# Column width of the routed experts' products, and where the routing tables are allotted

## The chip, the cores and the metric

The kernel runs on one core of a Trainium2 chip. The metric is the device time of one execution in microseconds (us); times below are medians of several executions. All data are fp32. The engines are TensorE (PE in the profile; its weight loads are shown apart as PEld), VectorE (DVE), ScalarE (ACT), GpSimd (POOL) and SyncE (SP, which issues most of the DMAs).

## The reference, cut to what matters

The reference is a decoder of two layers on `x` of 8 batches of 256 tokens with 256 features. Each layer has self attention, cross attention and a feed-forward part, each added to `x`. The change touches the end of layer 1: the start of its mixture of experts lies beside the last cross attention, and its routed experts are the last stage of the program. The mixture of experts, for 2048 tokens, 8 experts and F = 704:

```python
scores_aE = x_aD @ router_DE
vals_aK, idx_aK = jax.lax.top_k(scores_aE, K)                       # K = 1
gates_Ea = jax.nn.sigmoid(masked_aE).T                              # 0 for all other experts
routed_in_EaD = gates_Ea[:, :, None] * x_aD[None, :, :]
mid_EaF = silu(einsum('ead,edf->eaf', routed_in_EaD, w1_eDF)) * einsum('ead,edf->eaf', routed_in_EaD, w3_eDF)
routed_out_EaD = einsum('eaf,efd->ead', mid_EaF, w2_eFD)
shared_aD = silu(x_aD @ ws1_DF) * (x_aD @ ws3_DF) @ ws2_FD
out_aD = shared_aD + routed_out_EaD.sum(axis=0)
```

Since only one expert has a gate other than zero for a token, the kernel computes one expert per token.

## The kernel before, in words

The program works through the stages one after the other: layer 0, the self attention of layer 1, the cross attention of layer 1 with one batch at a time, and then the mixture of experts. A scheduler orders the instructions of an engine by priorities; where `tc.manual_schedule` is open, the engines it names keep the order in which the code records them. PE is under such a hand-written order around the projections of the cross attention (L1586, L1588) and in the stages after it, SP during the routed stage (L1884).

**Cross attention (`null_cross_attention`, from L1288).** For batch `b` the loop at L1568 records the scores (`stx`, L1431), their exponentials (`pTx`, L1435), the sums `both` (L1437, POOL), the denominators `den` (L1446) and the weighted values `ox` (L1470). While batch `b` is in work, the keys, values and queries of batch `b + 1` are made by `seven` (tiles `k`, `v`, `q`, products at L276). In the last batch there is no next batch, and the shared network of the experts takes that place: `load_shared` (L1054) loads `ws13` (weights ws1 and ws3, two DMAs at L1028 and L1029, and a small copy on POOL at L1030) and clears the tails of `mid0`, `mid1` and `ws2` (L1035, POOL); `hidden_shared` makes the first quarter of the shared hidden layer (`hx`, L1079), and DVE makes sums of the weights (`tws`, L1091). The reciprocals of the denominators (`rx`, L1490 and L1491, DVE) go to DRAM (`rd`, L1497) and back, spread over the partitions (`rs`, L1501); then `oT` is multiplied by them (L1525, POOL and DVE) and projected (`wo`, L276).

**Pools.** The projection weights of the cross attention and the keys, values and their sums lie in pools on the right side of SBUF that belong to `wproj`. `wproj.close()` at L1582 gives the room back, and the pool `mids` is opened in it. A first write into a new pool waits for the last readers of what lay in its room. In the kernel before, `mids` holds `ws13`, `mid0`, `mid1`, `ws2` and, by `routing_tables(late)` at L1604, all tables of the routing: index rows, `lower`, `run`, `sums`, `at`, `rank`, `hot`, `before` and some columns.

**Routed stage (`token_experts`, from L1644; loop in `slots`).** The tokens have been sorted by expert into 17 tiles of 128 rows. Twelve of them (numbers under `PAIRED` = 12) are full tiles of one expert. Five (12 to 16) are half tiles: 64 rows of one expert and 64 of another, with two sets of weights. They are taken in the order 0, 1, 12, 2, 3, 13, and so on. For each tile, SP loads `w13` (1408 KB for a set, L1808) two tiles ahead and `w2` (768 KB, L1815) one tile ahead, each kind with four buffers, so that a load waits until PE has read what lay in its buffer. Two tiles at a time are transposed on PE (`xrp`, L1824). `into` makes the hidden layer of the tile that comes next: 11 blocks of 128 hidden features, with two blocks of 128 input features each. `outof` multiplies the hidden layer (`midr`) by `w2`: 6 blocks into an output of 256 features (`out`, L1846). So PE runs `into` of tile i + 1 and then `outof` of tile i.

In `into` the products go through the helper `product` (L274 to L278), which splits the 128 columns of the stationary operand into two instructions of 64 columns that write partitions 0 to 63 and 64 to 127 of the output:

```python
nc.tensor.matmul(out[h], lhsT[:, h], rhs, start=start, stop=stop, skip_group_check=True)
for h in (slice(0, 64), slice(64, P))
```

`outof` splits in the same way. In a full tile both halves multiply the same `w2`; in a half tile each half, the 64 rows of one expert, multiplies its own. In `into` a half tile's 64 rows are the moving operand, so that its products have 128 columns of weights and 64 columns of tokens, once for each set. The hardware runs every fp32 product as two passes, each with a weight load of its own, so the profile counts twice the instructions that the code has: 88 for a full tile's `into`, 176 for a half tile's, 24 for `outof`.

After the last tile PE makes the last quarter of the shared network (`h`, L1079, and `out`, L1663), while POOL gathers the routed rows, and DVE adds them to `x`.

## Time and profile before

| | |
|---|---|
| median of 3 executions | 1196.16 us (1195.59 to 1197.24) |
| the profiled execution, its own time | 1198.71 us |
| its span, from the first to the last instruction | 1197.0 us |
| mean granted TensorE clock | 0.992 of full speed |
| PE busy | 1135.5 us, 95% of the span |
| weight loads busy | 706.5 us, 59% |
| DVE, ACT, POOL busy | 566.2, 447.5, 417.6 us |
| chain that ended last, by engine | PE 76%, POOL 7%, issue 6%, DVE 6%, ACT 4%, DMA 1% |
| `h` at L276, first products of the routed tiles | 87.0 us busy, 1936 passes |
| `out` at L1846, second products of the routed tiles | 47.1 us busy, 408 passes |

The profile is one execution. Busy times are unions of the records of an engine; the ends of matmuls are modelled and overlap, so the time that a group really takes is the distance between the start of its first instruction and the start of the next group, which the chain and the timelines show. The chain of waits follows the work back from the last instruction, at each step to what released it. In the lists of groups a line such as L276 may be that of a helper. A shape such as 128*64 128x128 gives the stationary operand (128 rows, 64 columns) and the moving one (128 rows, 128 columns).

### The profile page before, as it was taken

Reading aid. Unit: us, or ns where it says so; the run is one execution under the profiler, and the core shown is the slowest. Engines: PE = TensorE matmul, PEld = TensorE weight load, DVE = VectorE, ACT = ScalarE, POOL = GpSimd, SP = SyncE. Lnnn points to the kernel's source line nnn. Section 1 sums busy time; section 2 is a strip of 40 time slices with the busy share of each in tenths; the row PEclk is TensorE's granted clock in tenths of the full one; section 3 lists DMA queues with packets and bytes.
Section 4 is the critical chain, followed back from the end, with each engine's and each line's share of the span. In section 5 each row is a group of like instructions: output and inputs, shape, how many; then the busy total and the mean of one; then the engine's idle time right before and its main releaser. Section 6 shows DMA issues by size and latency. Waiting matters only on the chain.

```text
span 1197.0 us, 31939 instructions
## 1 busy us (share of the span) xinstructions
PE 1135.5 (95%) x13788; PEld 706.5 (59%) x13788; DVE 566.2 (47%) x1564; ACT 447.5 (37%) x696; POOL 417.6 (35%) x482
## 2 busy tenths in 40 slices
PE   6898899998899999999999999999998999999996
PEld 2334444454445454666676767666664576888864
DVE  5465878778685643824241424242324473222213
ACT  3666665665443541314141414141413230222220
POOL 3245365455655730314141414141415114100013
PEclk9999999999999999999999999999998999999999
DMA  7046232130200600020202010101103007799924
GB/s 226 1 133 204 91 119 92 54 122 2 84 2 17 233 3 19 2 54 2 54 2 54 6 50 10 46 19 37 24 15 105 5 30 305 277 414 394 392 73 129
DMA packets 51446, 116.78 MB, mean 98 GB/s; under 512 B 8272, under 2 KB 36416, under 8 KB 46944
## 3 DMA queue, kind: packets, MB, share of 16 engines
q1 hardware_dynamic: 45120, 98.90, 24.0%
q0 software_dynamic: 3456, 12.73, 2.9%
q10 hardware_dynamic: 2720, 3.02, 0.7%
q8 instruction: 110, 1.80, 0.6%
q14 instruction: 40, 0.33, 0.1%
HBM read 104.00 MB, written 27.93 MB: 110 GB/s over the span
## 4 chain that ended last, share of the span: by engine, by line
PE 76%; POOL 7%; issue 6%; DVE 6%; ACT 4%; DMA 1%; SPq 0%; POOLq 0%; ACTq 0%; DVEq 0%
PE h L276 7%; PE k L276 6%; PE v L276 6%; PE wo L276 5%; PE ox L1470 5%; PE stx L1431 5%; PE st L334 4%; PE out L1846 4%; PE o L371 3%; PE out L1663 3%; PE h L1079 3%; PE qk L282 3%; PE q L276 3%; ACT pT L345 2%; PE den L1446 2%
## 5 line engine op out<-in xcount | busy, mean ns | idle before, releaser
L345 ACT ACTIVATE pT<-st 128x1024 f32<-128x1024 f32 (+1 forms) x128 | 110.7, 919 | 64.3 <-PE st L334 64.3
L371 PE MATMUL o<-pT,padv 128*32 128x256 f32 (+1 forms) x1536 | 99.7, 370 | 4.3 <-POOL pT L350 4.2
L371 PEld LDWEIGHTS o<-pT,padv 128*32 128x32 f32 x1536 | 40.6, 109 | 86.2 <-issue 37.5
L1437 POOL TENSOR_TENSOR both<-pTx 128x512 f32<-128x512 f32 x64 | 81.2, 1296 | 29.0 <-ACT pTx L1435 23.8
L276 PE MATMUL h<-xrT,w 128*64 128x128 f32 (+1 forms) x1936 | 87.0, 250 | 0.4 <-issue 0.4
L276 PEld LDWEIGHTS h<-xrT,w 128*64 128x64 f32 x1936 | 84.4, 137 | 3.3 <-issue 1.1
L345 ACT ACTIVATE pT<-st,kbias 128x1024 f32<-128x1024 f32 x64 | 67.9, 1112 | 44.0 <-PE st L334 44.0
L258 POOL TENSOR_TENSOR lnrs<-lnve,mhalf 128x2 f32<-128x2 f32 x48 | 34.7, 723 | 127.8 <-DVE lnve L256 124.1
L1072 DVE TENSOR_TENSOR midr<-sl,h 128x128 f32<-128x128 f32 x102 | 29.4, 288 | 102.5 <-PE h L276 69.9
L1435 ACT ACTIVATE pTx<-stx 128x1024 f32<-128x1024 f32 x64 | 62.1, 1022 | 40.8 <-PE stx L1431 27.7
L1071 ACT ACTIVATE sl<-h 128x128 f32<-128x128 f32 (+1 forms) x114 | 35.4, 311 | 94.7 <-PE h L276 55.7
L334 PE MATMUL st<-qm,kT 32*128 32x512 f32 (+1 forms) x512 | 66.8, 591 | 4.0 <-ACT pT L345 2.0
L1431 PE MATMUL stx<-qTx,kTx 64*128 64x256 f32 x512 | 64.4, 391 | 2.5 <-ACT pTx L1435 2.5
L282 PE MATMUL qk<-l_wqkv,xnT 128*32 128x512 f32 x512 | 63.3, 607 | 0.7 <-ACT xnT L294 0.7
L1470 PE MATMUL ox<-pTx,vx 128*64 128x256 f32 x512 | 62.3, 385 | 0.0
L258 POOL TENSOR_TENSOR lxrs<-lxve,mhalf 128x2 f32<-128x2 f32 x8 | 5.6, 706 | 159.9 <-DVE sc L1210 124.2
L1525 POOL TENSOR_TENSOR oT<-oT,rs 128x512 f32<-128x512 f32 x30 | 37.3, 1273 | 65.0 <-DMA rs<-rd 65.0
L1431 PEld LDWEIGHTS stx<-qTx,kTx 64*128 64x128 f32 x512 | 46.1, 186 | 20.3 <-ACT pTx L1435 7.2
L276 PE MATMUL wo<-wout_x,oT 128*64 128x256 f32 x512 | 58.0, 379 | 0.0
L350 POOL TENSOR_SCALAR_AFFINE_SELECT pT<-pT 128x512 f32<-128x512 f32 x64 | 42.0, 670 | 41.8 <-ACT pT L345 38.7
L1846 PE MATMUL out<-w,midr 128*64 128x256 f32 x408 | 47.1, 379 | 2.7 <-issue 2.7
L1470 PEld LDWEIGHTS ox<-pTx,vx 128*64 128x64 f32 x512 | 33.9, 136 | 26.4 <-issue 12.5
(361 smaller groups left out, 2164.1 us busy)
## 6 DMA issues: line engine op xcount, KB each, us to landing
w<-packs SPq DMA_DIRECT2D x22, 1408.0 KB
w<-packs SPq DMA_DIRECT2D x22, 768.0 KB
rs<-rd SPq DMA_DIRECT2D x16, 512.0 KB
packs<-L_ffn_w_eDF SPq DMA_DIRECT2D x8, 704.0 KB
packs<-L_ffn_w_eDF SPq DMA_DIRECT2D x8, 640.0 KB
packs<-L_ffn_w_eFD SPq DMA_DIRECT2D x8, 640.0 KB
ctxT<-ctx_T SPq DMA_DIRECT2D x8, 512.0 KB
wkv_x<-L_xattn_Wkv POOLq DMA_DIRECT2D x1, 4096.0 KB
```

The source lines that it names most:

```text
L258: nc.gpsimd.tensor_tensor(rs[:, :n], ve[:, :n], mhalf[:, :n], ALU.pow)
L276: nc.tensor.matmul(out[h], lhsT[:, h], rhs, start=start, stop=stop, skip_group_check=True)
L282: nc.tensor.matmul(out[h : h + HP], lhsT[:, h : h + HP], rhs, start=start, stop=stop, skip_group_check=True)
L334: nc.tensor.matmul(st[:, r, :, :n], self.kT[rows, c, bass.ts(kt, P)], self.qm[rows, :, c, q0:], start=True, stop=True,)
L345: nc.scalar.activation(pT[:, :, :, :n], st[:, 2 * k : 2 * k + 2, :, :n], AF.Exp, scale=self.scale, **kb)
L350: nc.gpsimd.affine_select(out=pT[:, :, :, :P], in_=pT[:, :, :, :P], compare_op=ALU.is_ge, fill=0.0, base=0, pattern=[[0, 2], [0, 2], [1, P ...
L371: nc.tensor.matmul(o[HP * j : HP * j + HP, m, q0:], self.v_pad[:, kt, 8 * c + 2 * j + m, :], pTs[j // 2][:, j % 2, m, : S - q0], start=kt ...
L1431: nc.tensor.matmul(st[:, g, kt, :], kT[rows, c, bass.ts(kt, P)], qT[rows, c, :], start=True, stop=True)
L1435: nc.scalar.activation(pT, st, AF.Exp, scale=scale)
L1437: nc.gpsimd.tensor_tensor(both, pT[:, :, 0, :], pT[:, :, 1, :], ALU.add)
L1470: nc.tensor.matmul(o[XD * g : XD * (g + 1), i, :], v[:, kt, 2 * (c2 + i) + g, :], pT[:, g, kt, :], start=kt == 0, stop=kt == 1, skip_group ...
L1846: nc.tensor.matmul(ps[h], mid[:, i, h], sets[k % len(sets)][1][:, i, :], start=i == 0, stop=i == NFC - 1, skip_group_check=True,)
```

## The change

The first part opens a pool `route` after `mids` and allots the routing tables in it, so that `mids` becomes smaller. The second part writes the first products of all routed tiles with all 128 columns of weights in one instruction, and the second products of full tiles too. The second products of half tiles keep their two halves, since these have different weights.

```diff
                 late = ctx.enter_context(tc.tile_pool(name="mids", bufs=1, side="right"))
+                tables = ctx.enter_context(tc.tile_pool(name="route", bufs=1, side="right"))
                 load_shared(late)
                 sums = phase.enter_context(tc.tile_pool(name="sums", bufs=1, side="right"))
...
                 w_out(shared["ws2"], a["L1_ffn_ws2_FD"])
-                routing_tables(late)
+                routing_tables(tables)
...
             def first(h, lo):
                 for i, (w13, _) in enumerate(sets):
                     for c in range(2):
-                        product(h[:, bass.ts(i, n)], w13[:, c, lo : lo + P], xrT[:, c, bass.ts(i, n)], c == 0, c == 1)
+                        nc.tensor.matmul(
+                            h[:, bass.ts(i, n)],
+                            w13[:, c, lo : lo + P],
+                            xrT[:, c, bass.ts(i, n)],
+                            start=c == 0,
+                            stop=c == 1,
+                            skip_group_check=True,
+                        )
...
             for i in range(NFC):
-                for k, h in enumerate((slice(0, 64), slice(64, P))):
+                for k, h in enumerate((slice(0, 64), slice(64, P)) if len(sets) > 1 else (slice(0, P),)):
                     nc.tensor.matmul(
```

## Prediction

> **What bounds the kernel now.** I read the page first: TensorE (PE) is busy 95% of the span and holds 76% of the chain that ended last. A busy PE need not be at its limit, so I then read the chain of waits in order of time at the two places that the diff touches, the granted clock there, the weight loads (PEld) by shape, and the timelines of single groups. First place: the start of the shared network in the last batch of the cross attention (start us, length us, what).

> ```profile
> 915.49 4.35 DMA ws<-L_ffn_ws_DF
> 919.84 0.14 issue
> 919.98 6.62 PE hx L1079 x8
> 926.60 0.57 PE sc L276 x16
> 927.17 10.50 PE hx L1079 x24
> ```

> The load of ws13 is issued only at 915.49, and PE is idle for it from 916.56 to 919.98 (3.42 us). What follows is slow too: eight hx passes take 6.62 us where 24 take 10.50, 0.4375 each, so eight should take 3.50. The stretches tell why (stretch, length, busy us of PE, PEld, DVE, ACT, POOL, granted clock, DMA share, GB/s): after the pause PE runs at half clock.

> ```profile
> 918.00:920.00 2.00, 0.02 (x1) 0.06 (x1) 2.00 (x5) 0.00 (x0) 1.06 (x5) 0.77 1.01 397
> 922.00:924.00 2.00, 2.00 (x4) 0.83 (x3) 2.00 (x3) 0.00 (x0) 0.00 (x0) 0.50 1.14 360
> ```

> Second place: the routed stage, 1021 to 1158 us, again in the chain.

> ```profile
> 1042.20 0.59 PE xrp L1824 x4
> 1042.79 4.95 PE h L276 x88
> 1047.74 2.59 PE out L1846 x24
> 1050.34 4.80 PE h L276 x88
> ...
> 1130.43 5.13 PE h L276 x176
> 1135.56 2.10 issue
> 1137.65 2.81 PE out L1846 x24
> ```

> Each fp32 product is two passes, and each pass is today a pair of 64-column instructions side by side; I call the pair a slot. First products of a full tile: 4.80 / 44 = 109.1 ns a slot (128 tokens stream through). Of a half tile: 5.13 / 88 = 58.3 ns (64 tokens). Second products: 2.59 / 12 = 215.8 ns (256 columns). The middle of this stage:

> ```profile
> 1060.00:1098.00 38.00, 37.00 (x684) 33.19 (x682) 8.37 (x29) 10.40 (x35) 2.14 (x4) 1.00 1.00 401
> ```

> DMA is full as well, and PE waits for weights three times: the second products at 1063.60 last 3.37 us until the next group (2.59 undisturbed), the half tile at 1082.50 lasts 5.83 (5.13), and 2.10 are waited at 1135.56; together 3.6 us.

> What decides the case is the weight load by its width (line, shapes, count, busy us, mean ns, idle before):

> ```profile
> L282 PEld LDWEIGHTS back<-ys,put 128*32 128x32 f32 x256 | 8.7, 110 | 5.3 <-issue 0.7
> L276 PEld LDWEIGHTS h<-xrT,w 128*64 128x64 f32 x1936 | 84.4, 137 | 3.3 <-issue 1.1 <-ACT yr L1855 1.0 <-ACT sl L1071 0.2
> L1663 PEld LDWEIGHTS out<-ws,mid 128*128 128x128 f32 x192 | 36.3, 190 | 6.2 <-issue 1.0 <-ACT spx L1154 0.5
> ```

> From 32 to 64 columns a load grows by 27 ns, from 64 to 128 by 53: 0.83 ns a column. So 64 columns need 53 ns of loading and 128 need 106. A half tile's slot of 58.3 is the 64-column load and 5.3 ns, not the streaming: it is bound by loads, which two column halves make at once. And one place already runs 128-column fp32 products on short streams (start us, length us):

> ```profile
> 969.62 0.38 PE L1265 MATMUL counts<-hot,ones 128*128 128x128 f32 x2
> 969.84 0.39 PE L1266 MATMUL counts<-hot,lower 128*128 128x128 f32 x2
> 970.06 0.28 PE L1267 MATMUL counts<-low,ones 128*128 128x1 f32 x2
> ```

> and its weight loads:

> ```profile
> 969.95 0.30 PEld L1267 LDWEIGHTS counts<-low,ones 128*128 128x128 f32 x2
> ```

> Two passes over 128 tokens every 0.22 us, so 0.11 a slot. The last two loads cover 0.30 us, one lasts 0.19 (mean 192 ns): they start 0.11 apart although one column streams.

> [...]

> **The change part by part.**
> *First products of full tiles.* 12 tiles x 44 slots. By the load rule a 128-column slot is 106 + 5.3 = 111.3 ns (the counts show 0.11) instead of 109.1: +2.2 x 528 = +1.2 us. Bounds: 0, if streaming still sets it, and +1.6 at 112 ns.
> *First products of half tiles.* 5 tiles x 88 slots. 64 tokens still stream, but each slot has to load 128 columns through one path: 111.3 instead of 58.3 ns, +53.0 x 440 = +23.3 us. No product of 128 columns over 64 tokens is in the trace; bounds are 109 and 114 ns from the counts (+22.3 to +24.5), and, should loads overlap further, 58.3, that is no cost (first rival).
> *Second products of full tiles.* A 128-column pass over 256 columns in the shared products takes 18.13 / 84 = 215.8 ns (L1663 in the chain at 1000.24), the same as a pair today: 0. Its 106 ns load lies beside 216 ns of streaming.
> *Second products of half tiles* are unchanged.
> *Mode changes.* A turn into 64-column mode costs 0.15 us (4.95 - 4.80), a turn out 0.15 (four transposes 0.59 us against 0.43 at 1018.21, within 128-column mode). Before: one entry, eight rounds around transposes, one exit, 18 x 0.15 = 2.7. After: only around the second products of five half tiles, 10 x 0.15, and some 0.05 more each time the 128-column load comes back, 1.7. So -1.0 us (0 to -1.5).
> *Weight waits.* PE becomes slower while the 22 loads of each kind stay as they are, so the 3.6 us of waits go: -3.6 (0 to -3.6). What is late next is PE itself.
> The stage: +1.2 + 23.3 - 1.0 - 3.6 = +19.9 us.
> *Tables in their own pool.* In the built program ws13's load waited for the last ox product (done at 915.4); now it waits for the last product of batch 7's q (L276 q, ends at 895.5). So it is issued 20 us earlier into idle DMA queues and lands near 900 (4.35 us before). PE's pause and its half clock go: -(3.42 + 6.62 - 3.50) = -6.5 us. What moves with it: (a) SP: both parts of ws2 go ahead of rd; they wait for nothing after 895.5, and rd is due at 918.5. (b) POOL: three memsets (1.24 us at 915.5) move before lxrs and wait for the same q; ready at 896.8, when lxrs (896.84) is due. Behind them stand the normalization and the sums "both", for which den waits; a copy of 0.29 us also goes between these. The first two sums end at 905.3, 0.8 us before den at 906.07, so 0.4 us of delay is covered; without cover it would cost 0.4. (c) DVE: a tws of 0.74 us replaces an sx of 0.33 between rx and its reciprocal, so rd leaves 0.4 us later; in return rs no longer shares the queues with ws. Batch 6 needed 8.9 us from rd to oT (862.26 to 871.15), batch 7 11.1 (918.54 to 929.63). With 8.9 POOL's oT are ready at 930.4; wo now starts at 931.1. With 11.1 the second would be due 932.6, needed at about 933. Covered, by little: 0 to +1.
> All of the chain after 926 is PE's, or hangs on PE's products, and shifts along.

> Sum: +19.9 - 6.5 = +13.4 us. The profiled execution took 1198.71 us with a span of 1197.0, 2.55 above the median, so it should become 1212.1; from the median of 1196.16, 1209.6 us.

> **The rivals.** *Main case (0.85)*: as worked out. Bounds: +22.3 + 0 - 1.5 - 3.6 - 6.5 = +10.7, and +24.5 + 1.6 + 0 - 2.6 - 5.5 = +18.0 with 1 us of weight waits and 1 us of new stalls at wo left; 1207 to 1214.
> *Faster: loads of 128 columns hide behind short products (0.10).* Place: the half tiles' first products, at 58 to 60 ns a slot. For it: a wide load lies under a running product everywhere else, and transposes at 109 ns a slot (0.43 / 4) show no load cost at all. Against it: that stream is 128 long, and the L1267 loads keep 0.11. Then PE gains nothing, DMA stays the bound of the stage, and -6.5 to -7.5 remain: 1189. It decides below 81 ns a slot: there 440 x (81 - 58.3) = 10.0 us equals the 6.5 + 3.6 + 1.0 - 1.2 of gains.
> *The earlier load doesn't pay (0.03):* den or wo takes the place of the ws13 wait, and the pause returns there. Then +19.9: 1216. Against it are the margins above.
> *The clock falls in half tiles (0.02),* where only 64 of 111 ns stream: some of 49 us at half clock, 1225 and more. Against it: clock 1.00 at 58.3 ns slots today.

> **How the numbers follow.** The likeliest case gives 1209.6. Its bounds, 1207 to 1214, widened by 2 at the low end for the faster case's flank (a slot between 81 and 109), make the range 1205 to 1214; it leaves out the rivals, 0.15, and little of the main case. A difference under 0.2% (2.4 us) can't be told from none here. Faster by more: 0.10. Within: 0.02, a slot near 81 ns. Slower by more: 0.88.

> **What would show it.** Right: the half tiles' first products as 88 instructions over about 9.8 us (4.9 for full tiles), DMA share in the stage near 0.8, no wait for weights; hx starting at about 916.5 with clock 1.00 and ws13 issued near 895.6. Wrong: a half tile under 7 us, a DMA share still at 1.00, or a new pause at den, wo or the third group of hx (whose buffer DVE frees at about 923.2, 0.9 us before it is due).

## The result, and the profile after

The changed kernel takes 1210.54 us (median of 4 runs, 1207.61 to 1212.22), the kernel before 1196.21 (4 runs, 1195.59 to 1197.24): ratio 1.0126, interval 1.0102 to 1.0151. It is 14.3 us slower; +13.4 was forecast. The profiled execution took 1207.61 us with a span of 1205.9 and a mean clock of 0.997.

*The start of the shared network.* SP's timeline of the kernel after (start us, us, what):

```profile
893.93 0.40 SPq L1028 DMA_DIRECT2D ws<-L_ffn_ws_DF  x1
894.38 0.47 SPq L1029 DMA_DIRECT2D ws<-L_ffn_ws_DF  x1
...
917.13 1.28 SPq L1497 DMA_DIRECT2D rd<-rx  x4
```

The load of ws13 is issued 21 us before it is needed. The chain of waits of the same kernel:

```profile
913.59 0.57 PE den L1446 x8
914.16 0.59 PE tr L291 x4
914.75 3.44 PE hx L1079 x8
918.18 0.57 PE sc L276 x16
918.75 10.50 PE hx L1079 x24
929.25 7.95 PE wo L276 x72
```

No DMA and no pause stand between `tr` and `hx` any more, and the eight passes take 3.44 us where they took 6.62. A stretch within these eight passes (stretch, length, busy us of PE, PEld, DVE, ACT, POOL, granted clock, DMA share, GB/s) has the full clock, where the eight passes of the kernel before ran at 0.50:

```profile
916.00:918.00 2.00, 2.00 (x6) 0.63 (x4) 2.00 (x3) 0.00 (x0) 0.81 (x1) 1.00 0.01 2
```

`wo` starts 8.4 us earlier than before. Of this 1.8 us are not of the change: the last `den` already ends that much earlier, from differences that arise between 322 and 483 us, ahead of anything that was changed: there PE twice runs at half clock for 3.4 us in the profile before (from 322 and 475 us), and once in the profile after (from 397 us). So 6.6 us are the pool's.

*The routed stage.* The chain again, one round of it and the end:

```profile
1075.14 4.91 PE h L1837 x44
1080.05 2.59 PE out L1854 x12
1082.64 9.77 PE h L1837 x88
1092.41 2.65 PE out L1854 x12
...
1159.74 5.11 PE h L1837 x44
1164.85 5.18 PE out L1854 x24
1170.03 18.88 PE h L1079 x44
```

A full tile has 44 slots of 4.91 / 44 = 111.6 ns, a half tile 88 of 9.77 / 88 = 111.0 ns (58.3 before). From the first `h` at 1012.82 to the shared network at 1169.87 the stage takes 157.05 us; before it took 136.96 (1021.33 to 1158.29). That is +20.1. (With the products of before, the profiles of runs 1, 7, 9 and 10 have 134.8 to 139.0 us, depending on the waits in it; with those of after, runs 2 and 6 have 157.05 again.) Its middle, as a stretch:

```profile
1060.00:1098.00 38.00, 38.00 (x307) 35.79 (x306) 6.82 (x24) 9.04 (x30) 2.13 (x4) 1.00 0.80 307
```

PE never idles, the DMA share is 0.80 where it was 1.00 (over the whole stage 0.74 where it was 0.84), and the clock is full. The weight loads and products in the list of groups (busy us, mean ns of one, idle before):

```profile
L1837 PE MATMUL h<-xrT,w 128*128 128x128 f32 (+1 forms) x968 | 110.9, 275 | 0.0
L1837 PEld LDWEIGHTS h<-xrT,w 128*128 128x128 f32 x968 | 109.9, 192 | 1.5 <-issue 1.2
```

There are 968 loads of 128 columns where there were 1936 of 64. Together they are busy for 109.9 us, 113.5 ns for each, and PEld is idle for 1.5 us before them in all: one stands right behind the other, whether 64 or 128 tokens stream (111.0 and 111.6 ns a slot).

The spans of the two profiles differ by +8.9 us (1205.9 less 1197.0): -1.8 before the change's first place, -6.6 there, -0.1 between the two places, +20.1 in the routed stage, and -2.7 in the tail, from the shared network (`h`, L1079) to the end. The tail's part isn't the change's. The kernel before has a tail of 38.7 us, and the profiles of all ten experiments have 38.3 to 39.5, those of runs 2 and 6, with the same wide products, 39.1 and 39.3; only this one profile has 36.0. The change's own two parts give -6.6 + 20.1 = +13.5, and the medians +14.3.

### The profile page after: what moved, and what is told of

It reads as the page before. It is cut to its first block, busy times and chain, and to the rows that moved or that the text cites. A ratio compares the mean times of both kernels' runs of the same rounds, so it can differ in the third digit from the quotient of the medians.

```text
span 1205.9 us, 29715 instructions
## 1 busy us (share of the span) xinstructions
PE 1153.2 (96%) x12676; PEld 735.1 (61%) x12676; DVE 567.2 (47%) x1564; ACT 446.6 (37%) x696; POOL 418.2 (35%) x482
## 4 chain that ended last, share of the span: by engine, by line
PE 78%; POOL 6%; DVE 6%; issue 6%; ACT 4%; DMA 0%; POOLq 0%; ACTq 0%; DVEq 0%
PE h L1837 9%; PE k L276 6%; PE v L276 6%; PE wo L276 5%; PE ox L1470 5%; PE stx L1431 5%; PE st L334 4%; PE out L1854 4%; PE out L1664 3%; PE o L371 3%; PE qk L282 3%; PE h L1079 3%; PE q L276 3%; ACT pT L345 2%; PE den L1446 2%
## 5 line engine op out<-in xcount | busy, mean ns | idle before, releaser
L1837 PE MATMUL h<-xrT,w 128*128 128x128 f32 (+1 forms) x968 | 110.9, 275 | 0.0
L1837 PEld LDWEIGHTS h<-xrT,w 128*128 128x128 f32 x968 | 109.9, 192 | 1.5 <-issue 1.2
L1437 POOL TENSOR_TENSOR both<-pTx 128x512 f32<-128x512 f32 x64 | 82.1, 1309 | 27.0 <-ACT pTx L1435 23.2
L345 ACT ACTIVATE pT<-st,kbias 128x1024 f32<-128x1024 f32 x64 | 67.8, 1112 | 44.0 <-PE st L334 44.0
L1071 ACT ACTIVATE sl<-h 128x128 f32<-128x128 f32 (+1 forms) x114 | 35.3, 310 | 116.9 <-PE h L1837 75.5
L282 PE MATMUL qk<-l_wqkv,xnT 128*32 128x512 f32 x512 | 64.3, 615 | 0.7 <-ACT xnT L294 0.7
L276 PE MATMUL wo<-wout_x,oT 128*64 128x256 f32 x512 | 58.0, 379 | 0.0
L350 POOL TENSOR_SCALAR_AFFINE_SELECT pT<-pT 128x512 f32<-128x512 f32 x64 | 41.5, 661 | 41.4 <-ACT pT L345 38.3
L276 PEld LDWEIGHTS wo<-wout_x,oT 128*64 128x64 f32 x512 | 36.8, 137 | 18.4
```

The costliest lines, as they stand in the source:

```text
L282: nc.tensor.matmul(out[h : h + HP], lhsT[:, h : h + HP], rhs, start=start, stop=stop, skip_group_check=True)
L345: nc.scalar.activation(pT[:, :, :, :n], st[:, 2 * k : 2 * k + 2, :, :n], AF.Exp, scale=self.scale, **kb)
L350: nc.gpsimd.affine_select(out=pT[:, :, :, :P], in_=pT[:, :, :, :P], compare_op=ALU.is_ge, fill=0.0, base=0, pattern=[[0, 2], [0, 2], [1, P ...
L1437: nc.gpsimd.tensor_tensor(both, pT[:, :, 0, :], pT[:, :, 1, :], ALU.add)
L1837: nc.tensor.matmul(h[:, bass.ts(i, n)], w13[:, c, lo : lo + P], xrT[:, c, bass.ts(i, n)], start=c == 0, stop=c == 1, skip_group_check=True,)
```

## The experiments

The first four ran together on one chip, where the kernel before took 1198.49 us (11 runs, 1193.24 to 1203.36); the next four on one where it took 1198.76 (27 runs, 1195.70 to 1201.94). Ratios are to that. Theory: a slot of fp32 products lasts as long as the larger of its weight load (an estimate of 0.83 ns a column, from the growth of the mean record of a load, 110, 137 and 190 ns for 32, 64 and 128 columns) and its stream, and the pool takes away a pause and a slow clock (3.42 us, and 6.62 for 3.50). The rivals are named with each run.

**1. The pool alone.** The changed kernel with the products as before:

```diff
-                        nc.tensor.matmul(
...
+                        product(h[:, bass.ts(i, n)], w13[:, c, lo : lo + P], xrT[:, c, bass.ts(i, n)], c == 0, c == 1)
...
-                for k, h in enumerate((slice(0, 64), slice(64, P)) if len(sets) > 1 else (slice(0, P),)):
+                for k, h in enumerate((slice(0, 64), slice(64, P))):
```

> The tables' own pool alone; all routed products keep their 64-column halves. My theory (the earlier load of ws13 takes away 3.42 us of idle TensorE and 3.1 us at half clock, and the routed stage is untouched): 6.5 us less than before, about 1189.7 us; hx starts right after the transposes at clock 1.00, half tiles stay at 58.3 ns a slot and the stage at 137 us. Rival (the load is hidden anyway, den or wo takes over the wait): within 1 us of before, 1196.

Measured: 1192.13 us (1189.99 to 1195.19, 6 runs), ratio 0.9942 (0.9920 to 0.9964), so 6.4 us less by the medians (2.7 us either way by the interval). `hx` starts right behind the transposes here too. The pool's part of the forecast holds.

**2. The wide products alone.**

```diff
-                tables = ctx.enter_context(tc.tile_pool(name="route", bufs=1, side="right"))
...
-                routing_tables(tables)
+                routing_tables(late)
```

> The 128-column products alone; the tables stay in mids. My theory (half tiles' first products are bound by their weight loads at 111 ns a slot): the stage takes about 157 us instead of 137, 20 us more than before, about 1216 us, with the pause of 3.4 us ahead of hx still there. Rival (part of the loss of the changed kernel comes from the moved pool, its POOL and SP waits or other places in memory): 1211 or less.

Measured: 1219.25 us (1218.45 to 1221.19), ratio 1.0169 (1.0146 to 1.0193): +20.8. Its stage lasts 157.05 us, as in the kernel after. The two parts add up: -6.4 + 20.8 = +14.4, and together they gave +14.3 (each known to 3 us or so, so that the close agreement is luck). The pause ahead of `hx` is there with 3.39 us, but the eight passes behind it take 5.37 us and not 6.62, since the half clock lasts 3.4 us in this profile and 6.8 (from 919.1 us) in that of the kernel before. Against 3.50 at full clock that is 1.9 us in the one profile and 3.1 in the other.

**3. Half tiles' first products in pairs again.** Full tiles keep 128 columns; the pool stays.

```diff
+                        of = h[:, bass.ts(i, n)], w13[:, c, lo : lo + P], xrT[:, c, bass.ts(i, n)]
+                        if len(sets) > 1:
+                            product(*of, c == 0, c == 1)
+                        else:
+                            nc.tensor.matmul(*of, start=c == 0, stop=c == 1, skip_group_check=True)
```

> The changed kernel, but half tiles' first products in 64-column halves again; full tiles keep 128 columns. My theory (all of the cost but 1 us is the half tiles' weight loads): slots of 58.3 ns in half tiles, a stage near 137 us that waits for weights again, about 1190 us, within 1.5 us of the pool alone. Rival (the cost is in full tiles, or in leaving 64-column mode): the stage stays over 145 us and the time over 1198.

Measured: 1191.81 us (1189.22 to 1194.69), ratio 0.9945 (0.9924 to 0.9967). The stage takes 135.7 us, 21.3 less than in the kernel after, so the loss lies in the half tiles' first products. One part of the expectation failed: PE has no wait in this stage, where the pool alone has three of 3.5 us in all (stage 139.0), although the half tiles are as fast as there and the same weights come in a shorter time. Runs 9 and 10 take this up. The wide products of full tiles add a little to their slots (the section on the prediction has it), which the waits that are gone more than make up. This version beats both kernels and can't be told from the pool alone.

**4. Twice the loads, the same stream.** Each product over 64 tokens in half tiles becomes two over 32.

```diff
+                    m = n // len(sets)
+                    for k in range(len(sets)):
+                        cols = slice(i * n + k * m, i * n + (k + 1) * m)
```

> The changed kernel with each 128-column first product of a half tile over 64 tokens written as two over 32 tokens: the same result, the same number of streamed columns, twice the weight loads. My theory (the load sets the slot): 176 slots of 111 ns, 19.5 us for a half tile instead of 9.8, 49 us more than the changed kernel, about 1259 us. Rival (streaming and a fixed cost for each product set it, the load hides): a slot falls to 60 to 85 ns, 10.5 to 15 us for a half tile, 1214 to 1237 us.

Measured: 1342.80 us (1339.77 to 1343.64), ratio 1.1191 (1.1160 to 1.1223), some 130 us above the kernel after (each taken against the kernel before on its own chip), where 49 were expected. For its first 41 slots, 4.5 us, the first half tile runs as expected, 111 to 112 ns a slot. Then the next slots take 213 ns. Two stretches within one half tile:

```profile
1030.00:1040.00 10.00, 10.00 (x59) 10.00 (x58) 0.57 (x2) 0.28 (x1) 0.00 (x0) 0.61 0.52 216
1040.00:1050.00 10.00, 10.00 (x49) 10.00 (x48) 0.29 (x1) 0.55 (x2) 0.00 (x0) 0.50 0.00 0
```

PE counts as busy for all of it, yet the granted clock goes to 0.50. The timeline has the whole half tile:

```profile
1027.69 33.48 PE L1840 MATMUL h<-xrT,w 128*128 128x32 f32 x176
```

176 slots take 33.3 us, to the start of the next group, instead of 19.6. Here some 27 of 111 ns stream (an estimate from the 109.1 ns that 128 tokens took before). At full clock the slot keeps its 111 to 112 ns with half as many tokens, as the load theory has it; the expectation failed on the clock, which the next runs take up.

**5. Half tiles in four quarters of 32 columns.** The pool, full tiles in pairs, and less to load for each instruction (`product4` is the kernel's own helper for 32 columns).

```diff
+                        of = h[:, bass.ts(i, n)], w13[:, c, lo : lo + P], xrT[:, c, bass.ts(i, n)]
+                        if len(sets) > 1:
+                            product4(*of, c == 0, c == 1)
+                        else:
+                            product(*of, c == 0, c == 1)
```

> The tables' own pool, and the half tiles' first products each as four instructions over 32 columns, side by side; full tiles in pairs over 64 as before. If a slot costs the larger of its weight load and its stream, the load shrinks from 53 to 27 ns, so the 64 streamed tokens (about 54 to 56 ns) set the slot: 56 instead of 58.3, at most 1 us over the five half tiles, most of it hidden behind the transfers of weights. The time then falls by 6.5 to 7.5 us against before: ratio 0.994. Rival: what costs is the number of instructions that PE takes, and not the columns that each loads. Then four instructions take twice the time of two, about 116 ns a slot, and the stage loses what the kernel after loses: 25 us in half tiles, ratio above 1.01.

Measured: 1223.37 us (1218.01 to 1224.83), ratio 1.0194 (1.0172 to 1.0217). A miss of 31 us, and not for the rival's reason: where PE runs, a slot takes 55.8 ns (128 products in the second row below, start to start), as expected, and not 116. (58.3 with pairs, 2.5 ns more. That load and stream are nearly equal there is the author's estimate: 53 ns for 64 columns by 0.83 ns each, and half of 109.1 ns for 64 tokens.) But PE doesn't run all the time. Its timeline in the first half tile:

```profile
1028.55 1.76 PE L282 MATMUL h<-xrT,w 128*32 128x64 f32 x109
1031.53 1.99 PE L282 MATMUL h<-xrT,w 128*32 128x64 f32 x128 [1.22 <-issue]
1038.29 3.20 PE L282 MATMUL h<-xrT,w 128*32 128x64 f32 x115 [4.77 <-issue]
```

It stops after 109 products and again after exactly 128 more, and waits for nothing that is recorded on a semaphore. The wait of 4.77 us is followed by half the clock (3.20 us for 115 products). All ten such waits of the stage, 23.7 us, stand 109 to 115 past a multiple of 128 in PE's count of products. The DMA queue marked "instruction" (q8) moves pieces of 16,384 bytes: 110 in the kernel before with 13,788 products, 102 in the kernel after with 12,676, 117 here with 14,668. That is one piece for some 125 products and their loads, and the differences (-8 for -1112 products, +7 for +880) are one for 126 to 139. That a piece, called a block below, holds 128 products with their loads is an estimate from these counts and from the places of the waits. Between 1029 and 1034 us the list of DMA queues has one (packets, MB, share of 16 engines):

```profile
q8 instruction: 1, 0.02, 1.3%
```

One such transfer starts at 1029.06 and another only at 1035.72; each takes some 1.05 us, and PE goes on 1.4 and 1.5 us after they end. The author's reading is that PE ran out of instructions: it uses 128 products in 1.8 us. Beside the loads of weights the next piece started 4.2 us after PE had gone on (1031.53 to 1035.72), with the data queues empty 1.15 us after (1038.29 to 1039.44). The other eight waits are alike: with full queues 2.1 and 4.2 us, with queues empty or nearly so 1.1 to 1.2. That weights in the queues delay the pieces would fit, but no run separates it. The waits are 23.7 of the 31 us; the half clock behind some of them fits the rest (0.50 from 1038.50 to 1041.00 us).

**6. Longer streams, the same loads.** The changed kernel, the first set's products of half tiles over all 128 tokens:

```diff
+                    cols = slice(0, P) if i == 0 else bass.ts(i, n)
```

> The kernel after, where in half tiles the first set's products run over all 128 tokens instead of its 64 (what they put into the other 64 columns is overwritten by the second set's products). The same number of 128-column loads, one and a half times the streamed columns. Load theory: a slot stays at 111 to 112 ns, and the time is that of the kernel after within 1 us: ratio to before 1.012 to 1.013. Rival, that stream and load add up (53 of load and 54 of stream make the 111): 44 slots of each half tile grow by 53 ns, 2.3 us a tile, 11.7 us in all: ratio 1.022.

Measured: 1212.94 us (1210.27 to 1214.36), ratio 1.0117 (1.0096 to 1.0137). The same half tile in its timeline:

```profile
1027.68 9.93 PE L1838 MATMUL h<-xrT,w 128*128 128x128 f32 x88
1037.45 2.81 PE L1855 MATMUL out<-w,midr 128*128 128x256 f32 x12
```

(The shape in such a line is that of the group's first product; half of these still stream 64 tokens.) 88 slots in 9.77 us from start to start, as in the kernel after, with half as much again to stream. Load and stream didn't add up here: with 64 more tokens under half of the 128-column loads the slot stayed at 111.0 ns.

**7. The pause filled.** The kernel before, with products that nobody reads ahead of `hx`:

```diff
+                fill = mm.tile([P, 2 * S], F32, tag="mm", name="fill")
+                for _ in range(4):
+                    nc.tensor.matmul(fill, ident, shared["xnT"][:, 0, : 2 * S], start=True, stop=True)
```

> The kernel before, with four fp32 products of 128 x 512 put on PE where it waits for ws13 (eight passes of 0.43 us, 3.4 us in all, into a tile that nobody reads: work is added, none is left out). The load of ws13 stays late. Clock theory: PE doesn't pause, so hx starts at the same point but at full clock, and its first eight passes take 3.5 us instead of 6.6: 3.1 us less, ratio 0.9974. Rival: hx is slow there for what the transfers do, or since the first products after any wait for data are slow, not for the clock. Then nothing is gained, ratio 1.000, or above if the fill ends late.

Measured: 1196.29 us (1193.87 to 1201.91, 22 runs), ratio 0.9982 (0.9971 to 0.9993), 2.5 us less by the medians where 3.1 were expected. Its chain:

```profile
915.85 0.57 PE den L1446 x8
916.42 0.59 PE tr L291 x4
917.01 3.45 PE fill L1612 x8
920.46 3.65 PE hx L1079 x8
924.11 0.57 PE sc L276 x16
```

From the end of the last `ox` to the end of these `hx` passes it takes 8.26 us (915.85 to 924.11) instead of 11.17 (915.43 to 926.60): 2.9 less for 3.4 us of added work. The slow `hx` (6.62 us, 3.65 here) was the clock (0.50 there, 1.00 from 920 to 924 us here), and not the transfer beside it, which still runs (DMA share 0.76 in these 4 us).

**8. Three loads for two.** Between the kernel after and run 4: in half tiles only the second block of each contraction is cut in two.

```diff
+                        for lo_t in (i * n,) if c == 0 else range(i * n, i * n + n, m):
+                            cols = slice(lo_t, i * n + n if c == 0 else lo_t + m)
```

> The kernel after, where in half tiles the second half of each contraction is made in two products over 32 tokens instead of one over 64: the same result, three 128-column loads where there were two, the same streamed columns. Load theory at full clock: 132 slots of 111 ns in a half tile instead of 88, so 4.9 us more in each, 24.4 in all: ratio 1.033. Streaming covers 36 of 111 ns there on average (32%), between the kernel after (48%, clock 1.00) and the run with doubled loads (24%, clock fell to 0.50 after 5 us). If the clock falls here too, slots of 213 ns follow after some microseconds: a half tile takes some 25 instead of 14.6 us, 50 us more in all, ratio above 1.05.

Measured: 1296.14 us (1292.93 to 1299.62), ratio 1.0827 (1.0801 to 1.0852). The timeline and the stretches of the first half tile:

```profile
1028.39 24.05 PE L1840 MATMUL h<-xrT,w 128*128 128x64 f32 x132
```

```profile
1028.00:1032.00 4.00, 4.00 (x37) 3.95 (x35) 0.29 (x1) 0.65 (x2) 0.00 (x0) 1.00 1.03 428
1032.00:1040.00 8.00, 8.00 (x44) 8.00 (x43) 0.54 (x2) 0.56 (x2) 0.00 (x0) 0.56 0.49 198
```

The first slow slot comes 4.5 us after the group's start, as in run 4. In the five half tiles of each run it comes after 4.3 to 4.6 us in run 4 and after 3.7 to 6.5 in run 8. So with some 36 of 111 ns of streaming (32%, an estimate as in run 4) the clock went to 0.50, and with some 54 in the kernel after (48%, likewise) it stayed at 1.00. The rate of weight loads was nearly the same in all three while the clock was full: 35 (run 8) and 37 (run 4) from 1028 to 1032 us, 37 (kernel after) from 1026 to 1030. Whether the share of streaming decides, or the products over 32 tokens that only runs 4 and 8 have, these runs don't separate.

**9 and 10. The waits of the routed stage.** The prediction took three waits of the kernel before (3.6 us) for waits for weights. After run 5 there was another reading: blocks of instructions. In the kernel before the waits stand ahead of PE's products number 12146, 12529 and 13422 (114, 113 and 110 past a multiple of 128). To tell the two apart, instructions are added far ahead of the stage, in the pause of `hx`: 32 passes on the kernel before, 64 on the pool alone.

```diff
+                for _ in range(16):
+                    nc.tensor.matmul(fill[:, :P], ident, shared["xnT"][:, 0, :P], start=True, stop=True)
```

> The kernel before, with sixteen products over 128 columns (32 passes of 0.11 us, 3.5 us) where PE waits for ws13, into a tile that nobody reads: work is added, none is left out. It moves everything behind it 32 instructions on in PE's stream. In the profiles of the kernel before and of the pool alone PE's first wait in the routed stage stands in the middle of the second products of the second half tile, after 12 of 24; with eight more passes ahead (the filled pause) after 3 of 24. Instruction theory (PE waits for its next block of 128 products and their weight loads, which comes by DMA every 16,384 bytes): the wait, if there is one there, moves a further 24 earlier, into the first products of that half tile, 20 to 22 before their end, and every wait in the stage stands 109 to 116 past a multiple of 128 in PE's own count of products. Weight theory (my prediction): the waits stand where new weights are first used, at the start of first or second products, wherever that falls in PE's count. The time should be that of the filled pause, 1194 to 1197.

> The tables' own pool alone, with 32 products over 128 columns (64 passes of 0.11 us, 7.1 us) ahead of hx, into a tile that nobody reads: work is added, none is left out. Instruction theory: the waits of the routed stage stand 109 to 116 past a multiple of 128 in PE's count of products, so 64 products earlier in the work than with the pool alone (there before the 13th of 24 second products of the second half tile, within the first products of the third, and before those of the fifth). Weight theory: they stay at the same products. Time: 7 us above the pool alone, 1197 to 1200.

Measured: 1195.93 and 1199.66 us (one run each; the kernel before 1198.51 beside them). The first wait of the stage in the kernel before, by its timeline:

```profile
1063.43 1.47 PE L1846 MATMUL out<-w,midr 128*64 128x256 f32 x12
1065.46 1.51 PE L1846 MATMUL out<-w,midr 128*64 128x256 f32 x12 [0.56 <-issue]
```

in run 7, with 8 passes more ahead:

```profile
1060.94 0.60 PE L1849 MATMUL out<-w,midr 128*64 128x256 f32 x3
1062.68 2.54 PE L1849 MATMUL out<-w,midr 128*64 128x256 f32 x21 [1.14 <-issue]
```

and in run 9, with 32 more than the kernel before:

```profile
1055.97 4.76 PE L276 MATMUL h<-xrT,w 128*64 128x64 f32 x155
1062.24 0.81 PE L276 MATMUL h<-xrT,w 128*64 128x64 f32 x21 [1.51 <-issue]
```

The wait moves forward through the work by what was added behind it: from after 12 of 24 second products, to after 3, to 21 before the end of the first products. In PE's count it stays where it was: 12146, 12145, 12145. Run 9's other wait in the stage is at 13038 (110 past a multiple), those of run 10 at 11763 and 13039 (115 and 111). The first of run 10, in a list that leaves out the group's first 14 products:

```profile
1035.78 4.83 PE L276 MATMUL h<-xrT,w 128*64 128x64 f32 x159
1042.83 0.27 PE L276 MATMUL h<-xrT,w 128*64 128x64 f32 x2 [2.21 <-issue]
```

Each wait of the stage in these profiles and in run 5 ends 1.2 to 1.5 us after a piece of the instruction queue has landed (1.39, 1.28 and 1.23 in the kernel before). By place and by landing they are read as waits for instructions. PE didn't wait at every boundary (109 to 116 past a multiple of 128): at the places that were named ahead for run 10 there was no wait, so that this part of its expectation failed, and those that it had lay at other boundaries. None of the four waits of runs 9 and 10 lay off a boundary, and none at the start of a group that uses new weights. Run 3's one profile fits: with half as many instructions in full tiles alone PE didn't wait at all, though the weights were needed no later.

## Why the prediction was right, and where it wasn't

The sum was right: +13.4 forecast, +14.3 measured, 1209.6 against 1210.54. The stage, +19.9 forecast, grew by 20.1 in the profiles. One of its terms, the waits, came out by luck. Point by point:

- *First products of half tiles*, +23.3: the slot went to 111.0 ns (111.3 forecast, with 53 and 106 ns of loading as estimates from the mean records), 440 x 52.7 = 23.2 us, and the group behind each half tile takes 0.06 more (2.65 for 2.59), 0.3 in all. That a slot of 58.3 was "bound by loads" and not by streaming was only half so: in run 5, with half the columns to load, it still took 55.8. Runs 3 and 6 confirm cause and place: the stage is 21.3 us shorter when only these are in pairs, and with more streaming the half tile still took 9.77 us.
- *First products of full tiles*, +1.2: 111.6 less 109.1 ns, 528 times, 1.3 us. *Second products of full tiles*, 0: 2.59 us a tile, as before.
- *Mode changes*, -1.0: what remains shows in the chain. The half tiles' second products take 0.15 more (2.74), and then transposes take 0.59 where 0.44 is usual, or first products 5.11 for 4.91. That is 0.30 to 0.35 a half tile, 1.65 in all, where 1.7 was forecast (with an estimate of 0.05 for the load of 128 columns coming back).
- *Weight waits*, -3.6: the waits did go, and the size was right for that profile (those of runs 1, 7, 9 and 10 have 1.1 to 3.5 us of them). The cause was wrong. The prediction read "DMA is full as well, and PE waits for weights three times". The list of waits says only "issue" there, with no DMA named, and two of the three stood in the middle of a half tile's group, though such a group uses all of its weights (one transfer for each set) from its first block on. Runs 7 and 9 moved the first wait through the work and left it where it was in PE's count (12146, 12145, 12145), which fits a wait for instructions. By that reading the waits go as the same work now takes fewer instructions: a half tile's 176 products in 5.13 us, that is 128 in 3.7 us, became 88 in 9.77, and a full tile's 88 became 44 (in run 3's profile the full tiles' part alone went with no wait). The forecast came out right by luck, since both readings make a slower PE wait less. Run 5 is where they part: a faster slot with twice the instructions cost 31 us more than weights and slots alone allowed.
- *The pool*, -6.5: -6.6 at `wo` in the profile, -6.4 in run 1. Run 7, with 3.65 us at clock 1.00, shows that the 6.62 us were the clock after the pause; that they were 6.62 and not the 5.37 of run 2 belongs to the one profile. The side moves were covered: `wo` starts right behind `hx`, without a wait.
- *The rivals.* Loads of 128 columns didn't hide behind streams of 64 or 32 tokens (111.0 ns a slot in the kernel after, 111 to 112 in run 4). The earlier load did pay (run 1). The clock didn't fall in half tiles: with an estimated 54 of 111 ns streaming (48%; the prediction has 64) the kernel after kept 1.00, but in run 8, with an estimated 32%, it went to 0.50 within 7 us. Clock 1.00 at 58.3 ns a slot, the evidence given against it, didn't speak to that, since those slots stream nearly all the time (an estimated 54.6 ns, half of 109.1).
- "DMA stays the bound of the stage", in the faster rival, isn't what the profile shows: no wait of PE in that stage names a transfer of weights. A share of 1.00 here went with loads that ran ahead as buffers came free: in the kernel before SP waited 44.1 us for PE's `h` before it issued loads at L1808.

Open: how much of an instruction block's delay, if any, comes from the weights beside it; whether the share of streaming sets the clock, and if so where between the estimated 32 and 48% it falls; why the tail of the kernel after's one profile is short.

## What to carry to other kernels

For short fp32 streams compare the weight load of a slot with its stream: joining two 64-column halves into 128 columns cost 2% of a slot at 128 tokens (111.6 ns for 109.1) and nothing at 256 (2.59 us a tile in both), and made it 1.9 times as long at 64 (111.0 ns for 58.3). Before calling an "issue" wait one for data, look whether a transfer is named for it, and at its place in the engine's count of instructions: in run 5 quarters made the slot 2.5 ns shorter and brought 23.7 us of such waits. A load moved ahead is worth the pause and the slow clock behind it, here 3.4 us and 3.1 (1.9 in run 2's profile).
